# The flipped spectral product in 64 x 64 tiles with two PSUM banks

## The chip, the cores and the metric

The kernel runs on one core of a Trainium2 chip, as one program. The metric is device microseconds of that core from the launch's first to its last work, the median of three runs. TensorE is called PE here, its weight loads PEld, VectorE DVE, ScalarE ACT, GpSimd POOL and SyncE, which issues most DMAs, SP.

## The reference

Two layers on x of shape (4, 128, 64, 64) in float32: four images of 128 channels and 64 x 64 = 4096 tokens. The first layer is attention with four heads of 32 over the 4096 tokens, with projection, residual and a layer norm over the channels. The second takes that result and adds three branches:

```
spatial = conv_general_dilated(x, conv_spatial_w (3x3), padding 1) + bias
ym      = mamba(tokens of x)            # d_inner 256, 16 states, 4 taps
fft     = rfft2(x, axes=(-2, -1))
cat     = concatenate([fft.real, fft.imag], axis=1)
fc      = einsum("bchw,oc->bohw", cat, conv_spectral_w) + conv_spectral_b
fr, fi  = split(fc, 2, axis=1)
spectral = irfft2(complex(fr, fi), s=(h, w), axes=(-2, -1))
return spatial + spectral + ym
```

The spectral branch mixes channels in the frequency domain with a 256 x 256 matrix. Written out in the image domain, it is a channel mix of x, of a Hilbert transform of x along the rows, and of the same two with the image flipped in both directions. The part that goes to flipped positions is the one of this case: for a chunk of tokens, w = g_flip^T x + g_fliphil^T hilbert(x), with two 128 x 128 matrices.

## The kernel before, in words

**Chunks and steps.** The 4 x 4096 tokens are cut into 32 chunks of 512 (8 rows of an image). Attention sets the beat. A loop over t (from L1126 on) walks steps; 2048 of them do attention, 64 per chunk: two pairs of heads, 32 key tiles of 128 each. One step does, for 512 queries and 128 keys of two heads:

- L515 (`scores_for_exp`): the scores into bank pair `s2`, as pairs of matmuls with 64 contraction rows and 128 columns in float32r (one pass of the array), three pairs, the last from `MX`; ACT's exp reads them (L523, `e`).
- L474 (`scores_for_max`): the scores of another step once more into bank pair `s1`, two pairs of the same form; DVE's max reduce reads them (L481, `part`).
- L535 (`times_values`): `po` += V^T e, two matmuls in float32 on 128 rows and 33 columns. A float32 matmul stands in the trace as two MATMUL records (two passes), so this is four.

`s1` and `s2` have one buffer each, so L474 of a step waits for L481 of the step before, and L515 for L523.

**Products.** Everything else that PE does is small float32 products, through the helper `product` (L346): it splits the 128 output rows into two column tiles of 64, so each has 128 contraction rows and 64 columns. All such records carry line L349. PSUM's eight banks are two for `s1`, two for `s2`, one for `po`, one for the scan's `dA`, and two, `m0` and `m1`, which all the small jobs share.

**The planner.** The small jobs are generators. Each `yield` says what the next piece needs: "P" a PE place, "A" an ACT place, "D" a DVE place, "B" one of the two banks, and "" just another step. `Plan.step` (L125) runs in every step of attention; it goes through the jobs in the order of (rank, time, number) and advances each one at most by a piece that takes a bank, then on through pieces that need only "P" if places are left. Odd steps give two places each of P, A and D; even steps give one A place only (L1168, L1170). A bank comes back a step or two after `plan.release`. The engines' queues are in program order, so this order is the order on each engine. In an odd step the plan's products stand between L474 and L535 of that step on PE; on DVE, the jobs' work stands behind the reduce L481. On even steps DVE also does one row of the state scan (L884), POOL two or three multiplies for it.

**The jobs of a chunk.** `output_projection` (rank 0: `pa`, `py`, norm, `xh`), `mamba_input` (rank 1: transposes `pt`, then `xp`), which starts two `scan_input` (rank 1: `pi`, four taps on DVE, a sigmoid), `scan_bc` (rank 1: `pd`), two `scan_dt` (rank -1: `pdt`), `spectral` (rank 2), `gate` and `convolve` (rank 3: `pz`, `pf`), `scan_output` (rank 0: `py`), and the next image's `project_kv` and the next chunk's `project_q` (rank 0: `pk`, `pv`, `pq`). The state scan of a chunk is due 64 steps after its `mamba_input`.

**`spectral` (L925).** It takes a bank and a P place for `p1`, the Hilbert transform of `xh` on PE (tile `p` in the trace); ACT copies it to `hx` (L936). Then it takes a bank and a P place for `pw`: `product` with `g_flip` from the image tile `xp`; a P place, and `product` with `g_fliphil` from `hx` into the same bank. ACT copies the bank to `w` (L947), and SP writes `w` to DRAM (L951), from where `load_flipped` and `add_flipped` (L1010, L1023) take it for other chunks' outputs. `hx` is also read by `convolve`.

**The tail.** Attention ends some 220 us before the end; after it chunks 30 and 31 finish their scans, with more places per step (L1163) and POOL and DVE as the busy engines.

Of the kernel before, what the change touches and what calls it, by code (L numbers as in the profile page):

```python
# [11 lines left out]
AF = mybir.ActivationFunctionType  # L12
ALU = mybir.AluOpType
# [4 lines left out]
P = 128  # L18
W = 64
# [4 lines left out]
L = 512  # L24
RPC = L // W
# [136 lines left out]
def attention_then_conv_mamba(  # L162
# [17 lines left out]
    nc = tc.nc  # L180
    ctx.enter_context(tc.manual_schedule())
    B, C, N = x.shape
# [18 lines left out]
    for h in range(HEADS):  # L201
        k, j = divmod(h, 2)
# [3 lines left out]
    for h in range(HEADS):  # L206
        k, j = divmod(h, 2)
        c = COL["bk"] + k
# [8 lines left out]
    for h in range(HEADS):  # L217
        k, j = divmod(h, 2)
        c = COL["bq"] + h
# [36 lines left out]
    def col(name, k=0):  # L256
        return vec[:, COL[name] + k : COL[name] + k + 1]
# [12 lines left out]
    g_flip, g_hil, g_fliphil = (g[:, k, :] for k in range(3))  # L270
# [70 lines left out]
    rows = [slice(j * HS, (j + 1) * HS) for j in range(2)]  # L341
    used = [slice(j * HS, j * HS + HD + 1) for j in range(2)]

    plan = Plan(2, {"x": 2, "f": 1})

    def product(out, lhsT, rhs, start=True, stop=True):  # L346
        for q in range(2):
            cols = slice(q * HS, (q + 1) * HS)
            nc.tensor.matmul(out[cols], lhsT[:, cols], rhs, start=start, stop=stop)  # L349

    def bank_tile(bank, shape, name):
        return psum.tile(shape, F32, tag=f"m{bank}", name=name)
# [309 lines left out]
    def inner(c):  # L662
        return xps[c][:, 1 : RPC + 1, 1 : W + 1]

    def mamba_input(c):

        i = c % NCH
        while c not in XH:
            yield ""
        yield ""  # L670
        xp = loc.tile([P, RPC + 2, W + 2], F32, tag="xp", name=f"xp_{c}", bufs=2)
        xps[c] = xp
        nc.gpsimd.memset(xp[:, :, 0 : W + 2 : W + 1], 0.0)
        if i == 0:
            nc.gpsimd.memset(xp[:, 0, 1 : W + 1], 0.0)
            nc.gpsimd.memset(carry, 0.0)
        if i == NCH - 1:
            nc.gpsimd.memset(xp[:, RPC + 1, 1 : W + 1], 0.0)
        bank = yield "PB"
        pt = bank_tile(bank, [P, TPC, P], f"pt_{c}")  # L680
        for t in range(TPC):
            nc.tensor.transpose(pt[:, t, :], XH[c][:, t, :], ident)
        yield "A"
        plan.release(bank)
        nc.scalar.activation(
            inner(c),
            pt.rearrange("p t (r w) -> p (t r) w", w=W),
            AF.Identity,
            scale=col("gamma"),
            bias=col("beta"),  # L690
        )
        if i:
            nc.scalar.activation(xp[:, 0, 1 : W + 1], xps[c - 1][:, RPC, 1 : W + 1], AF.Copy)
            nc.scalar.activation(xps[c - 1][:, RPC + 1, 1 : W + 1], xp[:, 1, 1 : W + 1], AF.Copy)
            edges.add(c - 1)
        if i == NCH - 1:
            edges.add(c)

        xss[c], dts[c], us[c] = {}, {}, {}
        for hf in range(NH):  # L700
            plan.now(1, scan_input(c, hf))
        plan.now(2, spectral(c))

    def scan_input(c, hf):

        bank = yield "PB"
        pi = bank_tile(bank, [P, RPC, W], f"pi_{c}_{hf}")
        product(pi, inw[:, hf * P : (hf + 1) * P], inner(c))
        yield "A"
        plan.release(bank)  # L710
        xi = loc.tile([P, L + TAPS - 1], F32, tag=f"sg{hf}", name=f"xi_{c}_{hf}", bufs=1)
        nc.scalar.activation(xi[:, : TAPS - 1], carry[:, hf, :], AF.Copy)
        nc.scalar.activation(xi[:, TAPS - 1 :], pi.rearrange("p r w -> p (r w)"), AF.Identity)
        nc.scalar.activation(carry[:, hf, :], xi[:, L:], AF.Copy)
        s = loc.tile([P, L], F32, tag=f"xs{hf}", name=f"xs_{c}_{hf}", bufs=1)
        bank = yield "DB"
        ps = bank_tile(bank, [P, L], f"conv_{c}_{hf}")
        nc.vector.tensor_scalar(
            ps, xi[:, :L], col("c1_w", hf * TAPS), col("c1_b", hf), ALU.mult, ALU.add
        )  # L720
        for k in range(1, TAPS):
            yield "D"
            nc.vector.scalar_tensor_tensor(
                s if k == TAPS - 1 else ps,
                xi[:, k : k + L],
                col("c1_w", hf * TAPS + k),
                ps,
                ALU.mult,
                ALU.add,
            )  # L730
        plan.release(bank, 2)
        a = yield from sigmoid(s, f"sg{hf}", f"{c}_x{hf}")
        nc.gpsimd.tensor_tensor(s, s, a, ALU.mult)  # L733
        yield ""
        xss[c][hf] = s
        if len(xss[c]) == NH:
            plan.now(1, scan_bc(c))
# [187 lines left out]
    def spectral(c):  # L925

        b, i = divmod(c, NCH)
        bank = yield "PB"
        p1 = bank_tile(bank, [P, TPC, P], f"p1_{c}")
        for t in range(TPC):  # L930
            product(p1[:, t, :], XH[c][:, t, :], hilbert)
        yield "A"
        plan.release(bank)
        hx = loc.tile([P, L], F32, tag="hx", name=f"hx_{c}", bufs=2)
        hxs[c] = hx
        nc.scalar.activation(  # L936
            hx, p1.rearrange("p t c -> p (t c)"), AF.Copy, scale=col("gamma")
        )
        bank = yield "PB"
        pw = bank_tile(bank, [P, RPC, W], f"pw_{c}")  # L940
        product(pw, g_flip, inner(c), True, False)
        yield "P"
        product(pw.rearrange("p r w -> p (r w)"), g_fliphil, hx, False, True)
        yield "A"
        plan.release(bank)
        w = loc.tile([P, L], F32, tag="w", name=f"w_{c}", bufs=1)
        nc.scalar.activation(w, pw.rearrange("p r w -> p (r w)"), AF.Copy)  # L947
        yield ""
        if i == 0:
            wd[b] = dram.tile([P, N], F32, tag="wd", name=f"wd_{b}")  # L950
        nc.sync.dma_start(wd[b][:, i * L : (i + 1) * L], w)  # L951
# [162 lines left out]
    for c in range(CHUNKS):  # L1114
        t0 = (c + 1) * SLOT
        plan.at(t0, 0, load_residual(c))
        plan.at(t0 + 16, 1, mamba_input(c))
        plan.at(t0 + SLOT + 30, 3, convolve(c))
        plan.at(c * SLOT + LAG + 6, 3, gate(c))
        plan.at((c + 1) * SLOT + LAG + (2 if c < CHUNKS - 3 else 6), 0, scan_output(c))  # L1120
# [7 lines left out]
    while t < end or not plan.idle():  # L1128
# [10 lines left out]
        c, s = divmod(t - LAG, SLOT)  # L1139
# [110 lines left out]
```

## Time and profile before

| What | Value |
|---|---|
| Median of 3 runs | 5814.76 us (5813.01 to 5815.22) |
| Profiled execution, its own time | 5816.46 us |
| Span from first to last instruction in it | 5814.7 us |
| Mean granted TensorE clock | 0.986 |
| PE busy / DVE / ACT / POOL | 97% / 75% / 61% / 79% |
| `pw<-xp,g` on PE | 128 records of 632 ns mean |
| `pw<-hx,g` on PE | 128 records of 605 ns mean |
| `w<-pw` on ACT (L947) | 32 of 590 ns |
| `hx<-p` on ACT (L936) | 32 of 684 ns |

The profile is of one execution. A row of groups names line, engine, operation, the tiles out<-in, the tile of the array as contraction rows * columns (64*128), out and in shapes, and the count. PE records overlap, so a group's cost is read from its start to the next group's start.

### The profile page before, as it was taken

To read this page: it belongs to the slowest core of one execution; us is meant where nothing else is said; L and a number is where in the kernel's file an instruction comes from. 1 tells how busy PE (TensorE), PEld (TensorE's weight loads), DVE (VectorE), ACT (ScalarE), POOL (GpSimd) and SP (SyncE) were. 2 spreads that over 40 slices of the span, in tenths; PEclk is the share of its full clock that TensorE was granted. 3 is DMA by queue.
4 is the path that set the end of the run, shared out by engine and by line. 5 is a ranking of instruction groups with operands and counts; after the bars stand their busy time and mean duration, and the time that the engine had idled before them with its cause. 6 is when DMAs were issued, how large, how long until landed. Compare 5 with 4: busy or idle time off the path is not lost. (4 is left out here: it accounts for less than half of the span.)

```text
span 5814.7 us, 89440 instructions
## 1 busy us (share of the span) xinstructions
PE 5614.2 (97%) x33642; PEld 2423.7 (42%) x33642; DVE 4357.9 (75%) x4665; ACT 3518.5 (61%) x4794; POOL 4578.1 (79%) x4659
## 2 busy tenths in 40 slices
PE   5999999999999999999999999999999999999976
PEld 2444444444444444444444444444444444444421
DVE  4557777777777777777777777777777777777768
ACT  1455666666666666666666666666666666666653
POOL 0006888888888888888888888888889888888987
PEclk7999999999999999999999999999999999999988
DMA  4012233333333232333433323332433222232233
GB/s 133 22 32 64 68 76 77 74 73 111 87 94 80 74 73 77 75 71 87 110 89 83 81 69 74 80 76 70 113 78 96 71 69 66 69 73 69 66 98 93
DMA packets 424880, 456.81 MB, mean 79 GB/s; under 512 B 203872, under 2 KB 207488, under 8 KB 424448
## 3 DMA queue, kind: packets, MB, share of 16 engines
q1 hardware_dynamic: 419792, 449.23, 30.9%
q8 instruction: 265, 4.34, 0.3%
q10 hardware_dynamic: 4656, 1.87, 0.1%
q14 instruction: 167, 1.37, 0.1%
HBM read 376.21 MB, written 66.32 MB: 76 GB/s over the span
## 5 line engine op out<-in xcount | busy, mean ns | idle before, releaser
L481 DVE TENSOR_REDUCE part<-s 128x2 f32<-128x1024 f32 x2048 | 2500.7, 1222 | 1300.1 <-PE s L474 1295.7
L523 ACT ACTIVATE e<-s 128x1024 f32<-128x1024 f32 x2048 | 2097.1, 1024 | 1977.9 <-PE s L515 1968.1
L535 PE MATMUL po<-e,V 128*33 128x512 f32 x8192 | 2145.1, 602 | 11.3 <-ACT oz L546 11.3
L515 PE MATMUL s<-Q,K 64*128 64x512 f32 x8192 | 1502.5, 444 | 29.6 <-ACT e L523 26.0
L515 PEld LDWEIGHTS s<-Q,K 64*128 64x128 f32 x8192 | 610.6, 185 | 1754.8 <-ACT e L523 1330.0
L474 PE MATMUL s<-K,Q 64*128 64x512 f32 x8192 | 1309.1, 396 | 30.8 <-DVE part L481 19.3
L894 POOL TENSOR_TENSOR hs<-hs,bc 128x512 f32<-128x512 f32 x948 | 1215.1, 1282 | 138.5 <-DVE hs L884 70.2
L872 POOL TENSOR_TENSOR db<-u,bc 128x512 f32<-128x512 f32 x948 | 1218.1, 1285 | 0.0
L913 POOL TENSOR_TENSOR acc<-acc,hs 128x512 f32<-128x512 f32 x894 | 1146.9, 1283 | 70.1
L884 DVE TENSOR_TENSOR_SCAN hs<-dA,state,db 128x512 f32<-128x512 f32 x826 | 1052.6, 1274 | 51.0 <-ACT dA L867 48.8
L474 PEld LDWEIGHTS s<-K,Q 64*128 64x128 f32 x8192 | 769.1, 185 | 252.2 <-DVE part L481 64.7
L515 PE MATMUL s<-MX,sel 64*128 64x512 f32 x4096 | 814.4, 392 | 0.0
L867 ACT ACTIVATE dA<-dt,negA 128x512 f32<-128x512 f32 x1024 | 702.4, 686 | 91.6 <-DVE V L884 79.2
L535 PEld LDWEIGHTS po<-e,V 128*33 128x33 f32 x8192 | 339.9, 109 | 761.6 <-issue 706.0
L893 POOL COPY state<-hs 128x1 f32<-128x1 f32 x858 | 160.1, 187 | 526.6 <-DVE hs L884 526.1
L515 PEld LDWEIGHTS s<-MX,sel 64*128 64x128 f32 x4096 | 390.5, 184 | 93.6 <-issue 0.4
L349 PE MATMUL pf<-d,cw 128*64 128x256 f32 x1536 | 195.1, 384 | 0.0
L579 POOL TENSOR_TENSOR op<-op,rz 128x512 f32<-128x512 f32 x32 | 41.6, 1299 | 176.6 <-DMA rz<-rd 176.6
L884 DVE TENSOR_TENSOR_SCAN hs<-dA,zero,db 128x512 f32<-128x512 f32 x128 | 163.1, 1274 | 1.2 <-POOL db L872 1.0
L349 PE MATMUL acc<-V,cst 128*64 128x512 f32 x280 | 91.1, 748 | 67.8 <-POOL V L894 67.3
L349 PEld LDWEIGHTS pf<-d,cw 128*64 128x64 f32 x1536 | 102.0, 136 | 100.4 <-issue 59.1
L733 POOL TENSOR_TENSOR xs<-xs,sg_x 128x512 f32<-128x512 f32 x64 | 82.1, 1282 | 74.0 <-ACT sg_x L657 74.0
(158 smaller groups left out, 3455.7 us busy)
## 6 DMA issues: line engine op xcount, KB each, us to landing
bc<-bcd SPq DMA_DIRECT2D x487, 512.0 KB
Q<-qd SPq DMA_DIRECT2D x256, 128.0 KB
K<-kd SPq DMA_DIRECT2D x64, 256.0 KB
MX<-md SPq DMA_DIRECT2D x1024, 0.5 KB
K<-bcd SPq DMA_DIRECT2D x42, 256.0 KB
vd<-vst SPq DMA_DIRECT2D x32, 264.0 KB
V<-vd SPq DMA_DIRECT2D x32, 264.0 KB
xq<-in_x SPq DMA_DIRECT2D x32, 256.0 KB
```

Source lines behind the costliest of these rows:

```text
L349: nc.tensor.matmul(out[cols], lhsT[:, cols], rhs, start=start, stop=stop)
L474: nc.tensor.matmul(sc[:, j, :], QT[H][rows[j], n, t * P : (t + 1) * P], KK[k][m][rows[j], :], start=n == 0, stop=n == 1,)
L481: nc.vector.tensor_reduce(part[H][:, :, t, m], sc, AX.X, ALU.max)
L515: nc.tensor.matmul(s[:, j, :], sel[rows[j], :] if n == 2 else KK[k][i][rows[j], t * P : (t + 1) * P], mov[rows[j], :], start=n == 0, stop= ...
L523: nc.scalar.activation(e, s, AF.Exp)
L535: nc.tensor.matmul(po[H][used[j], :], VA[i][:, t, 2 * k + j, :], e[:, j, :], start=m == 0, stop=m == NT - 1,)
L867: nc.scalar.activation(dA[c, v], dts[c][hf], AF.Exp, scale=negA[:, k : k + 1])
L872: engine.tensor_tensor(db[c, v], us[c][hf], bcs[c, n][0], ALU.mult)
L884: nc.vector.tensor_tensor_scan(hs, dA.pop((c, v)), db.pop((c, v)), state[:, k : k + 1] if c % NCH else zero, ALU.mult, ALU.add,)
L893: nc.gpsimd.tensor_copy(state[:, k : k + 1], hs[:, L - 1 :])
L894: nc.gpsimd.tensor_tensor(hs, hs, bcs[c, n][1], ALU.mult)
L913: nc.gpsimd.tensor_tensor(accs[c, hf], accs[c, hf], hs, ALU.add)
```

## The change

The flipped product no longer goes through `product`. Each of the two factors is cut into two halves of the contraction (rows 0 to 63 and 64 to 127) and two halves of the output columns, so into four tiles of 64 x 64. The two halves of the contraction go into two different banks, `pw[0]` and `pw[1]`; each bank collects both factors. Eight matmuls in all, in the order factor, row half, column half, take the place of four. They are issued together on one P place. ACT copies the first bank to `w` as before, and DVE adds the second bank to `w`, on a D place of its own; `w` goes to DRAM as before. The job asks for its first bank without a place ("B"), keeps it, and asks for the second with the P place ("PB"). Its rank in the planner goes from 2 to 1.

```diff
-        plan.now(2, spectral(c))
+        plan.now(1, spectral(c))
...
-        bank = yield "PB"
-        pw = bank_tile(bank, [P, RPC, W], f"pw_{c}")
-        product(pw, g_flip, inner(c), True, False)
-        yield "P"
-        product(pw.rearrange("p r w -> p (r w)"), g_fliphil, hx, False, True)
-        yield "A"
-        plan.release(bank)
+        banks = [(yield "B"), (yield "PB")]
+        pw = [bank_tile(k, [P, L], f"pw{r}_{c}") for r, k in enumerate(banks)]
+        for first, lhsT, rhs in ((True, g_flip, inner(c)), (False, g_fliphil, hx)):
+            for r in range(2):
+                for q in range(2):
+                    nc.tensor.matmul(
+                        pw[r][rows[q]],
+                        lhsT[rows[r], rows[q]],
+                        rhs[rows[r]],
+                        start=first,
+                        stop=not first,
+                    )
+        yield "A"
+        plan.release(banks[0])
         w = loc.tile([P, L], F32, tag="w", name=f"w_{c}", bufs=1)
-        nc.scalar.activation(w, pw.rearrange("p r w -> p (r w)"), AF.Copy)
+        nc.scalar.activation(w, pw[0], AF.Copy)
+        yield "D"
+        plan.release(banks[1], 2)
+        nc.vector.tensor_tensor(w, pw[1], w, ALU.add)
```

## The prediction

> **What bounds the kernel now.** I read the page's busy shares and its 40 slices first:
>
> ```profile
> PE 5614.2 (97%) x33642; PEld 2423.7 (42%) x33642; DVE 4357.9 (75%) x4665; ACT 3518.5 (61%) x4794; POOL 4578.1 (79%) x4659
> PE   5999999999999999999999999999999999999976
> DVE  4557777777777777777777777777777777777768
> PEclk7999999999999999999999999999999999999988
> ```
>
> PE is at 90% or more in every slice but the first and the last two; DVE has about a quarter free in between. A busy PE may still be waiting behind itself, so I went to PE's timeline around one product that the change touches:
>
> ```profile
> 1084.37 0.63 PE L474 MATMUL s<-K,Q 64*128 64x512 f32 x4
> 1084.92 1.05 PE L535 MATMUL po<-e,V 128*33 128x512 f32 x4
> 1085.91 0.73 PE L515 MATMUL s<-Q,K 64*128 64x512 f32 x4
> 1086.48 0.39 PE L515 MATMUL s<-MX,sel 64*128 64x512 f32 x2
> 1086.71 0.63 PE L474 MATMUL s<-K,Q 64*128 64x512 f32 x4
> 1087.27 1.08 PE L349 MATMUL pw<-xp,g 128*64 128x512 f32 x4
> 1088.18 1.03 PE L349 MATMUL pw<-hx,g 128*64 128x512 f32 x4
> 1089.04 1.03 PE L535 MATMUL po<-e,V 128*33 128x512 f32 x4
> 1089.99 0.73 PE L515 MATMUL s<-Q,K 64*128 64x512 f32 x4
> 1090.57 0.40 PE L515 MATMUL s<-MX,sel 64*128 64x512 f32 x2
> 1090.80 0.63 PE L474 MATMUL s<-K,Q 64*128 64x512 f32 x4
> ```
>
> The first number is the start. Read start to start, because the ends overlap the next group. One attention step, from an L474 group to the next, is 1086.71 - 1084.37 = 2.34 us; the step with the two `pw` products is 1090.80 - 1086.71 = 4.09 us. So the flipped product costs 4.09 - 2.34 = 1.75 us of PE, with no gap in it. Of 32 chunks, 31 run it in such a step (the last one, at 5670 us, is in the tail): 31 x 1.75 = 54 us, 0.9% of the time, is all that the PE side can give. Last, PE's own waits on other engines inside these steps:
>
> ```profile
> PE s L515 <- ACT e L523: 26.0, 49, 0.8
> PE s L474 <- DVE part L481: 19.3, 29, 1.3
> PE po L535 <- ACT oz L546: 11.3, 35, 0.3
> ```
>
> That is 57 us in all, 1.8 us per chunk: attention steps are bound by PE's own throughput, not by waits.
>
> **Part 1, the rate inside the product.** `pw<-hx` takes 0.86 us to the next group (1089.04 - 1088.18) with four records of about 0.59 us each: two column tiles, each f32 matmul in two passes. Two tiles run side by side: the records start in pairs (1087.268 and 1087.275, then 1087.749 and 1087.756), so one pass of 512 columns is 0.86 / 2 = 0.43 us, whatever the number of tiles beside it. After the change, each of the two factors is four tiles of 64 x 64, eight records. Row halves side by side are shown by L515 and L474 (two 64-row tiles per pair), column halves by L349; both at once by no row. If all four run together, a factor is again 2 x 0.43 = 0.86 us: the same arithmetic on the same array. If only two at a time, it is 1.72 us, +1.72 us for both factors. If a 64-row tile streamed a pass in half the time, it would be 0.43 us, -0.86 us for both. I take four together: both halvings are seen separately, and the array is fully covered before and after, so no cells lie idle that the new tiles could use. A small loss: the L515 `MX` pair, row tiles with 512 columns in one pass, takes 1086.71 - 1086.48 = 0.23 us, against 0.215 per half-length of a column pass (0.86 / 4). If row tiles lose this 0.015 us in each of the four passes, that is 0.06 us per chunk.
>
> [...]
>
> **Part 2, the change of tile shape.** The timeline has a price for it. Two pairs of L474 alone are 2 x 0.23 = 0.46 us, but from L474 to `pw` it is 1087.27 - 1086.71 = 0.56: 0.10 us for the change. The first `pw` group then takes 0.91 instead of 0.86: 0.05 us of weight load with nothing to hide it. From `pw` to `po`, both 128-row column tiles, nothing is paid (0.86); into `po` from `s` it costs 0.99 - 0.86 - 0.10 (the exit) = 0.03 of weight load and 0.10 of change. So now there are two changes a step, s to pw and po to s. With 64 x 64 tiles there are three: s to pw, pw to po, po to s. The added one is 0.10 + 0.03 = 0.13 us per chunk. Bounds: if `s` to 64 x 64 is no change, because both have 64 rows, 0.15 us goes and this term is -0.02; if another product comes ahead of `pw` in its step (the P place that the change frees allows it), one more change of 0.15 is added: +0.28. I take 0.13: every pair of unlike shapes that stand next to each other in this trace pays.
>
> [...]
>
> **Part 3, the eviction.** Removed: nothing on ACT (one copy of 128x512 before, L947, 590 ns, and one after, from bank 0). Added on DVE: a 128x512 add of PSUM and SBUF. The same form is in the trace:
>
> ```profile
> L1061 DVE TENSOR_TENSOR ob<-ym,py 128x512 f32<-128x512 f32 x32 | 21.7, 678 | 2.8 <-PE py L349 2.8
> ```
>
> So 0.68 us x 32 = 22 us on DVE, which goes from 75% to 75.3%. What hides it is DVE's idle time ahead of the reduce that frees the max scores' bank:
>
> ```profile
> 1093.82 1.23 DVE L481 TENSOR_REDUCE part<-s 128x2 f32<-128x1024 f32 x1
> 1094.96 0.68 DVE L655 SCALAR_TENSOR_TENSOR sg_z<-zg,ln_z 128x512 f32<-128x512 f32 x1
> 1097.05 1.23 DVE L481 TENSOR_REDUCE part<-s 128x2 f32<-128x1024 f32 x1 [1.42 <-PE s L474]
> ```
>
> In the very step after the `pw` eviction DVE does one 0.68 us job and then idles 1.42 us; a second one fits. Behind the add, if its wait for PE or ACT ran late, stand that reduce and, behind the reduce, PE's next L474. Where the add meets a full DVE (the plan lets two D jobs into one odd step), all 0.68 us reach PE: 31 x 0.68 = 21 us. From below: 0. I take 0, with 0.7 us for the one chunk in the tail, where DVE is busy 93.9 of the last 114 us. The write of `w` to DRAM now waits on DVE instead of ACT; behind it on SP's queue are Q and bc loads issued steps ahead of use, so I cost this at nothing; a late one would show as a PE wait, of which L474 on Q has 0.7 us now.
>
> **Part 4, banks and order.** The plan has two banks for all small jobs. The spectral job now takes one, keeps it while it waits for the other, and then holds both until ACT and DVE have read them: for two to four steps no other bank job starts. Its rank goes from 2 to 1, so it passes `scan_bc`, and it needs one P place fewer. This moves jobs by steps, but the state scan of a chunk is due 64 steps after its `pt` (L1117 and LAG), and in the trace `pd` and the last `pdt` come 65 and 83 us after `pt` (1093.7 and 1111.4 against 1028.4), some 24 and 31 steps at the 172.6 us from one `pt` to the next; so none should come late. What a move can do is put an ACT or DVE job beside or away from a full step. Now that costs PE, per chunk, 26.0 / 32 = 0.8 us at L515 and 19.3 / 32 = 0.6 at L474. One wait of about 0.7 us more or less per chunk is 31 x 0.7 = 22 us up or down. I take 0: no row says which.
>
> **The sum.** Per chunk 0.06 + 0.13 = 0.19 us; 31 x 0.19 = 5.9, with 0.7 in the tail 6.6 us. The profiled execution took 5816.5 us (span 5814.7): 5823.1. The median of the runs is 1.7 lower, 5814.76, so the forecast is 5821 us, +0.1%.
>
> **Rivals.**
> - *Slower, two tiles at a time* (the change doesn't do what it says): +1.72 x 31 + 6.6 = +60 us, 5875. For it: no row has four tiles at once. Against: paired starts for both halvings. It decides as soon as the four first-pass records of a factor don't start within a few tens of ns. Chance 0.12.
> - *Slower, DVE or the banks become a wait of PE* in about every chunk: 0.4 to 1 us x 31 on top of the sum, +19 to +38, about 5843. For it: L474 waits for DVE already 29 times, once per chunk. Chance 0.17.
> - *Faster, the moved jobs take away one of PE's waits*: -22 + 6.6 = -15, 5800. Chance 0.08.
> - *Faster, a 64-row pass is half as long*: -0.86 x 31 + 6.6 = -20, 5795. Chance 0.03; nothing speaks for it but that L474's 64-row passes take 0.23, and those also make one pass where these f32 products make two.
> - *The forecast*, +0 to +11 us: chance 0.60.
>
> A difference under 0.2% (11.6 us) is about what a measurement of this kernel can't tell from none. Faster 0.11, within 0.60, slower 0.29. The forecast's own range is 5810 to 5826. From 5794 to 5852 the range takes in both faster cases and nearly all of the DVE one; left out are the two-at-a-time case and little else.
>
> **What the profile after would show.** Part 1: sixteen `pw` records per chunk, form 64*64, each group of eight 0.85 to 0.95 us to the next; 1.7 means two at a time. Part 2: `po` after `pw` starting 0.1 late and its first pass 0.03 longer; the step with `pw` at about 4.28 instead of 4.09. Part 3: a new DVE group of 32 at 0.68 us, and PE's wait for L481 still near 19 us. Part 4: PE's wait for L523 still near 26 us. The prediction is wrong if one of the last two moves by more than 10 us, or if the `pw` groups aren't 0.9 us.

## The result, and the profile after

The changed kernel takes 5869.64 us (5867.65 to 5872.63), against 5814.69 before (four runs): ratio 1.0095, 95% interval 1.008 to 1.011. The forecast was 5821, its range ended at 5852. The profiled execution took 5871.4 us, 55.0 more than that of before. The page after, the same lines as before:

```profile
PE 5643.0 (96%) x33898; PEld 2422.4 (41%) x33898; DVE 4374.3 (75%) x4697; ACT 3516.2 (60%) x4794; POOL 4572.5 (78%) x4659
PE   6999999999999999999999999999999999999976
PEclk7999999999999999999999999999999999999988
```

PE has 256 records more (8 per chunk) and only 29 us more of busy time; its share even fell. So the page says little; the timeline says more. First PE around one changed product (the x4 line is the same place in a window cut 0.4 us behind its start):

```profile
1100.40 0.63 PE L474 MATMUL s<-K,Q 64*128 64x512 f32 x4
1100.96 1.09 PE L944 MATMUL pw<-xp,g 64*64 64x512 f32 x8
1101.87 1.03 PE L944 MATMUL pw<-hx,g 64*64 64x512 f32 x8
1102.84 1.05 PE L535 MATMUL po<-e,V 128*33 128x512 f32 x4
```

```profile
1100.96 0.66 PE L944 MATMUL pw<-xp,g 64*64 64x512 f32 x4
```

Four records start at once (1100.959 to 1100.979 singly), and each factor of eight records takes 0.91 and 0.97 us to the next group, where before had 0.91 and 0.86. So all four tiles run together, and nothing is seen of a cost of row tiles. The exit into `po` shows the added change of shape: 0.97 - 0.86 = 0.11. The add on DVE, by group, and where it falls in time:

```profile
L957 DVE TENSOR_TENSOR w<-pw,w 128x512 f32<-128x512 f32 x32 | 21.9, 683 | 3.6 <-ACT w L954 2.3 <-PE pw L944 1.3
```

```profile
1109.47 0.68 DVE L957 TENSOR_TENSOR w<-pw,w 128x512 f32<-128x512 f32 x1
1110.88 1.23 DVE L481 TENSOR_REDUCE part<-s 128x2 f32<-128x1024 f32 x1 [0.73 <-PE s L474]
```

Behind this add DVE still idles 0.73 us. So neither the tiles nor, in this step, the add is where 55 us went. PE's waits on others point elsewhere (us in total, times, longest):

```profile
PE s L515 <- ACT e L523: 42.4, 105, 0.7
PE po L535 <- ACT oz L546: 20.3, 63, 0.3
PE s L474 <- DVE part L481: 18.6, 28, 1.3
```

Against 26.0, 49 times, and 11.3, 35 times, before: about twice as many waits for the exp and for `oz`. `oz` is the copy of a finished `po`, which happens at each change of head pair, every 32 steps. By the steps in which they fall, before has 29 of the waits for the exp and 30 of those for `oz` behind the second change of a chunk (steps 33 and 34), and 0 and 3 behind the first. After has the same behind the second and adds 56 and 27 behind the first (steps 1 to 3). Here is the first step behind such a change at the start of a chunk (step 1 of its 64): PE before, ACT before, then PE, ACT and DVE after:

```profile
1994.99 0.74 PE L515 MATMUL s<-Q,K 64*128 64x512 f32 x4
1995.56 0.40 PE L515 MATMUL s<-MX,sel 64*128 64x512 f32 x2
1995.79 0.63 PE L474 MATMUL s<-K,Q 64*128 64x512 f32 x4
1996.35 1.08 PE L349 MATMUL pf<-hx,g 128*64 128x512 f32 x4
1997.26 1.03 PE L349 MATMUL pf<-d,cw 128*64 128x256 f32 x8
1998.12 1.03 PE L535 MATMUL po<-e,V 128*33 128x512 f32 x4
1999.08 0.73 PE L515 MATMUL s<-Q,K 64*128 64x512 f32 x4
```

```profile
1996.10 0.59 ACT L546 ACTIVATE oz<-po 33x512 f32<-33x512 f32 x1 [1.27 <-DVE oz L545]
1997.11 1.01 ACT L523 ACTIVATE e<-s 128x1024 f32<-128x1024 f32 x1
```

```profile
2011.71 0.73 PE L515 MATMUL s<-Q,K 64*128 64x512 f32 x4
2012.27 0.40 PE L515 MATMUL s<-MX,sel 64*128 64x512 f32 x2
2012.51 0.62 PE L474 MATMUL s<-K,Q 64*128 64x512 f32 x4
2013.47 1.05 PE L535 MATMUL po<-e,V 128*33 128x512 f32 x4 [0.33 <-ACT oz L546]
2014.89 0.73 PE L515 MATMUL s<-Q,K 64*128 64x512 f32 x4 [0.37 <-ACT e L523]
```

```profile
2012.82 0.59 ACT L546 ACTIVATE oz<-po 33x512 f32<-33x512 f32 x1 [1.40 <-DVE oz L545]
2013.32 0.58 ACT L802 ACTIVATE lnw<-u 128x512 f32<-128x512 f32 x1
2013.84 1.00 ACT L523 ACTIVATE e<-s 128x1024 f32<-128x1024 f32 x1
```

```profile
2010.84 1.23 DVE L481 TENSOR_REDUCE part<-s 128x2 f32<-128x1024 f32 x1 [2.01 <-PE s L474]
2012.09 0.70 DVE L545 COPY oz<-po 33x512 f32<-33x512 f32 x1
```

Read it from the bottom. DVE copies its half of `po` only behind a reduce (2012.09), ACT's half waits for that (2012.82), PE's next `po` waits for ACT (2013.47, 0.40 later than the usual 0.56 behind L474), and the exp, third in ACT's queue, holds the next L515 by 0.43. Before, two products of the convolution (`pf`, 1.75 us of PE) stood in just this step: the copy ended at 1996.69, well ahead of PE's `po` (1998.12), and the exp at 1998.12, ahead of the next L515 (1999.08), so nothing waited. After, the products aren't there.

**Where the 55 us are.** For every attention step I took the time from its first L515 record to the next step's, and took off the price of what stands in it: 2.348 us for the step and 0.87 to 0.885 per product, the medians of steps without waits. The sum of what is left over (the excess, us, from chunk 1 on; "K" are other steps with over 0.8 us each):

| Steps of the 64 in a chunk | before | after |
|---|---|---|
| 0 to 2, first change of head pair | 5.3 | 36.0 |
| 32 to 34, second change of head pair | 33.6 | 33.6 |
| K, mostly the load of a new image's keys, three times | 10.1 | 19.4 |
| the `pw` step itself | -0.5 | 3.7 |
| all others | 12.9 | 21.2 |
| sum | 61.4 | 113.9 |

Of the 52.5 us between the sums, 30.7 are the first line. (PE's two wait lines above grew by 25 only: they count from the modelled end of the record before, start to start counts all.) Another 2.7 us come in the tail; no cause is known for them. The order of the products tells the reason of the first line. Steps in which they stand in PE's queue, from 49 on into the next chunk (so in 21 of the 31 chunks; before, step 1 holds two products in 28 of the 31, after in none):

```
before  49 pw  51 pd  53 pf+pf  55 pdt+pf  57 pdt  61 pz           1 pf+pf  3 pq+pf   5 pf
after   53 pw  55 pd  57 pz     59 pdt+pdt         61 pf+pf 63 pf  7 pq    11 pf+pf  13 pa+pf  15 pf
```

In the plan of after, which the planner's code gives without a run, the spectral job takes its first bank in step 49, where before it issued `pw`; the second is held by the gate's logarithm until 52, so `pw` comes in 53. `pd` goes from 51 to 55, `pz` passes the convolution, the convolution starts eight steps late, and step 1 stays empty. The rank alone does nothing of this: in the plan with only the rank changed, PE's instructions stand in the same order as before (no run was made of it).

### The profile page after: what moved, and what is told of

Read it like the earlier page. It is cut to its first block, busy times and chain, and to the rows that moved or that the text cites. A ratio compares the mean times of both kernels' runs of the same rounds, so it can differ in the third digit from the quotient of the medians.

```text
span 5869.6 us, 89999 instructions
## 1 busy us (share of the span) xinstructions
PE 5643.0 (96%) x33898; PEld 2422.4 (41%) x33898; DVE 4374.3 (75%) x4697; ACT 3516.2 (60%) x4794; POOL 4572.5 (78%) x4659
## 5 line engine op out<-in xcount | busy, mean ns | idle before, releaser
L481 DVE TENSOR_REDUCE part<-s 128x2 f32<-128x1024 f32 x2048 | 2499.4, 1221 | 1273.2 <-PE s L474 1269.4
L523 ACT ACTIVATE e<-s 128x1024 f32<-128x1024 f32 x2048 | 2093.4, 1022 | 1983.9 <-PE s L515 1980.1
L535 PE MATMUL po<-e,V 128*33 128x512 f32 x8192 | 2147.8, 603 | 20.5 <-ACT oz L546 20.3
L515 PE MATMUL s<-Q,K 64*128 64x512 f32 x8192 | 1503.6, 445 | 47.5 <-ACT e L523 42.4
L474 PE MATMUL s<-K,Q 64*128 64x512 f32 x8192 | 1313.2, 398 | 34.6 <-DVE part L481 18.6
L515 PEld LDWEIGHTS s<-Q,K 64*128 64x128 f32 x8192 | 611.1, 185 | 1779.4 <-ACT e L523 1327.7
L872 POOL TENSOR_TENSOR db<-u,bc 128x512 f32<-128x512 f32 x948 | 1215.3, 1282 | 0.0
L884 DVE TENSOR_TENSOR_SCAN hs<-dA,state,db 128x512 f32<-128x512 f32 x826 | 1053.1, 1275 | 106.2 <-POOL db L872 59.9
L474 PEld LDWEIGHTS s<-K,Q 64*128 64x128 f32 x8192 | 767.8, 186 | 267.4 <-DVE part L481 74.5
L515 PE MATMUL s<-MX,sel 64*128 64x512 f32 x4096 | 813.6, 393 | 0.0
L515 PEld LDWEIGHTS s<-MX,sel 64*128 64x128 f32 x4096 | 388.0, 184 | 93.0 <-issue 0.6
L884 DVE TENSOR_TENSOR_SCAN hs<-dA,zero,db 128x512 f32<-128x512 f32 x128 | 163.2, 1275 | 7.9 <-POOL db L872 7.7
```

The source lines that it names most:

```text
L474: nc.tensor.matmul(sc[:, j, :], QT[H][rows[j], n, t * P : (t + 1) * P], KK[k][m][rows[j], :], start=n == 0, stop=n == 1,)
L481: nc.vector.tensor_reduce(part[H][:, :, t, m], sc, AX.X, ALU.max)
L515: nc.tensor.matmul(s[:, j, :], sel[rows[j], :] if n == 2 else KK[k][i][rows[j], t * P : (t + 1) * P], mov[rows[j], :], start=n == 0, stop= ...
L523: nc.scalar.activation(e, s, AF.Exp)
L535: nc.tensor.matmul(po[H][used[j], :], VA[i][:, t, 2 * k + j, :], e[:, j, :], start=m == 0, stop=m == NT - 1,)
L872: engine.tensor_tensor(db[c, v], us[c][hf], bcs[c, n][0], ALU.mult)
```

## The experiments

Theory A: the moved order leaves attention's own waits at a change of head pair without work to cover them; the tiles cost 4 us. Rivals: B, the 64 x 64 shape is the cost; C, the DVE add is; D, the bank kept idle is, wherever the products stand. The kernel before was run again beside each set of experiments (medians 5815.12 us for 1 to 4, 5815.9 for 5 to 8, 5816.55 for 9 and 10); the ratios are to these.

**1. Old tile shape in the new order.**

```diff
+        product(pw[0].rearrange("p (r w) -> p r w", w=W), g_flip, inner(c))
+        product(pw[1], g_fliphil, hx)
```

in place of the loop of eight matmuls.

> The kernel after, with its two banks, its places, its rank and its DVE add, but with the old tile shape: the factor g_flip goes into the first bank and g_fliphil into the second, each through the helper in tiles of 128 rows by 64 columns. Theory A (lost cover: the moved order of the small products leaves attention's own waits open, and the tile shape itself costs 0.13 us per chunk): 5870 less 31 x 0.13 = 4, about 5866. Theory B (the 64 x 64 shape is what costs): back near 5815 to 5820. Theory C (the DVE add or the reads of two banks cost): 5866 as in A, so this run doesn't part A from C.

Measured 5861.61 us, ratio to before 1.0078 (1.0063 to 1.0093). B falls: with the old tiles 47 of the 55 us stay. The first line of the table is 35.7, the `pw` step -0.5 again. From the first to the last attention step it is 4.8 us less than after, 4.2 of them in the `pw` step, which is the tiles; the other 3 us of the difference of medians lie in the tail and ahead of the first step, and I have no cause for them.

**2. The cover taken away from before.**

```diff
-            plan.step(t, {"D": 2, "P": 2, "A": 2})
+            plan.step(t, {"D": 2, "P": 0 if t % SLOT == 1 else 2, "A": 2})
```

> The kernel before, with nothing changed but that the plan gives no PE place in step 1 of every chunk's 64 (t % 64 == 1), the odd step behind the change of head pair; the convolution's product that stood there moves to step 3. No work is added. Theory A: the wait at that step opens, about the 31 us by which the excess over the sum of the products grew at that step from before to after: 5840 to 5848. Theory B and C: 5815 within 5.

Measured 5845.77 us, ratio 1.0052 (1.0037 to 1.0067). Before, with its one bank, its tiles and no added work, is 31 us slower when step 1 has no product. The excess at steps 0 to 2 goes from 5.3 to 36.7, that at all others stays. This is A's mechanism by itself.

**3. Products moved into the two steps, in after.** The same line of the plan, with `0 if t % NT == NT - 1 else 2`.

> The kernel after, with 64 x 64 tiles and two banks, but the plan gives no PE place in the last odd step ahead of each change of head pair (t % 32 == 31). That moves one convolution product from step 63 to step 1 and one input product from step 31 to step 33. No work is removed. Theory A: each stands in a wait of about 1.1 us with 0.88 us of PE work, so 0.7 to 0.9 us comes back at each of the two steps: 31 x 2 x 0.8 = 50, about 5820. Theory B and C: 5870 within 5, since tiles, eviction and amount of work are the same.

Measured 5826.01 us, ratio to before 1.0018 (1.0009 to 1.0028): 44 us back, with tiles, banks and add as in after. A expected 50. PE at step 1 and the step behind it now:

```profile
1994.93 0.62 PE L474 MATMUL s<-K,Q 64*128 64x512 f32 x4
1995.49 1.08 PE L349 MATMUL pf<-d,cw 128*64 128x256 f32 x8
1996.40 1.03 PE L535 MATMUL po<-e,V 128*33 128x512 f32 x4
1997.36 0.74 PE L515 MATMUL s<-Q,K 64*128 64x512 f32 x4
1998.72 1.05 PE L535 MATMUL po<-e,V 128*33 128x512 f32 x4
1999.97 0.50 PE L515 MATMUL s<-Q,K 64*128 64x512 f32 x2 [0.19 <-ACT e L523]
```

One product of 0.88 us covers the first wait, and a second, 0.19 us, stays a step later. Excess 36.0 to 21.0 at steps 0 to 2, 33.6 to 4.5 at 32 to 34. The miss against A's 50 is mostly in steps 0 to 2: in ten of the 31 chunks (the first three and the last seven) no product came into step 1, which leaves 7.9 us, and step 2 keeps 8.3.

**4. The same rule in before.**

> The kernel before with the same rule (no PE place where t % 32 == 31). Only the input product moves, from step 31 to step 33, where before has an open wait of about 1.1 us in each chunk (33.6 us in all). Theory A: 31 x 0.8 = 25 us faster, about 5790. Theory B and C say nothing of it: 5815.

Measured 5787.63 us, ratio 0.9952 (0.9938 to 0.9967): 27 us faster than before. The second change of head pair had been open in both kernels; 33.6 goes to 4.6.

**5. Both banks in one piece**, up to chunk 22. The planner learns a need with two B's and serves it when two banks are free (its own lines are left out here):

```diff
-        banks = [(yield "B"), (yield "PB")]
+        if c < CHUNKS - NCH - 1:
+            banks = yield "PBB"
+        else:
+            banks = [(yield "B"), (yield "PB")]
```

> The kernel after, but up to chunk 22 the flipped product takes its two banks in one piece, when both are free, instead of keeping the first for four steps while it waits for the second. By the plan it then runs in step 49, as before, and the input of the scan follows in step 51; but the convolution still comes late, and step 1 of a chunk still holds no product. Theory A (what counts is which steps hold a product): the wait behind step 1 stays, about 31 us, and only the smaller waits go, of which the load of K (9 us) is the largest: 5850 to 5862. Theory D (the bank kept idle is the cost, wherever the products come to stand): about three quarters of the 50 us go, 5830 or less.

Measured 5845.05 us, ratio 1.0049 (1.0034 to 1.0064), 5 us under A's range and 15 above D's. Steps 0 to 2 keep 34.8 us, as A said, since `pz` and not the convolution comes last and step 1 is empty still. The K line went from 19.4 to 8.9 and the others fell by 10, more than I had counted. So taking the first bank early costs about 24 us, through these and 4 us of the tail, and is not the cause of the largest part.

**6. Both copies of `po` on ACT**, in after.

```diff
-            nc.vector.tensor_copy(oz[H][used[1], :], p[used[1], :])
+            nc.scalar.activation(oz[H][used[1], :], p[used[1], :], AF.Identity)
```

> The kernel after, with both halves of po copied to oz by ACT (L545 moves from DVE to ACT). The order of the products is untouched. If the open wait behind a change of head pair is the chain reduce on DVE, copy on DVE, copy on ACT, PE's next po and ACT's next exp, then ACT's two copies of 0.59 us start as soon as po ends, po is free about 0.3 us sooner, and the exp about as much: 31 x 2 x 0.3 to 0.5 = 19 to 31 us faster than after, 5839 to 5851. If the wait has another source (the load of Q, the P places), 5870 within 5.

Measured 5838.37 us, ratio 1.0037 (1.0024 to 1.005), 31 us faster than after. Both changes of head pair lose about 12 us (36.0 to 23.6, 33.6 to 21.9), and the wait of `po` for `oz` is all but gone from PE's lines (20.3 to 0.3). So DVE's late copy is about a third of the excess. What is left is PE's wait for the exp, which didn't fall (42.4 to 42.6): in the step that I read, at 1828 us, the exp stands behind both copies and L802 on ACT, and PE's next L515 waits 0.38 us for it. The other 7 us came in smaller waits, 5 of them in step 12.

**7. The add left out.** The line of the DVE add is taken away, its place in the plan stays.

> The kernel after with the DVE add left out, so that w holds only one half of the contraction; the place for it in the plan and both banks' times are kept. Theory A: the add lies in DVE's idle time, 5870 within 4. Theory C: the add is the cost, about 5820 to 5830.

Measured 5869.24 us, ratio 1.0089 (1.0074 to 1.0104): as after. C falls, and the 22 us of DVE work cost nothing.

**8. Experiment 4 with both copies on ACT.**

> The kernel before with no PE place where t % 32 == 31, as in the run that was 27 us faster than before, and both copies of po on ACT. Each change of head pair has a product in its wait now, so little is left for the second edit: 5780 to 5788.

Measured 5784.16 us, ratio 0.9944 (0.9927 to 0.996). That is 3 us under experiment 4, which was run in another set; the two intervals overlap, so nothing is shown of a second gain. As expected, what is covered has little left to give.

**9 and 10. The whole cover given back to after.** The plan's line once more, with no P place in steps 61 and 63, and in the second kernel none in 31 either.

> The kernel after, with no PE place in steps 61 and 63 of a chunk's 64, so that the two first convolution pieces (1.75 us of PE work) move together into step 1, the one behind the change of head pair where before had 1.74 us of products. No work is removed; nothing of the tiles, banks or the add is touched. Theory A: the wait of step 1 is covered wholly, as before: 30 of the 36 us there come back, 5836 to 5842. Theory B, C: 5870 within 5.

> As the run before it, and with no PE place in step 31 either, which moves one input product into step 33. Theory A: 30 us at step 1 and 29 us at step 33 come back: 5807 to 5813, at or under the kernel before, with the change still in.

Measured 5832.3 us (ratio 1.0026, 1.0016 to 1.0035) and 5810.46 us (0.9987, 0.9978 to 0.9997). In the first, PE at step 1:

```profile
1997.97 0.62 PE L474 MATMUL s<-K,Q 64*128 64x512 f32 x4
1998.53 1.95 PE L349 MATMUL pf<-d,cw 128*64 128x256 f32 x16
2000.30 1.03 PE L535 MATMUL po<-e,V 128*33 128x512 f32 x4
2001.26 0.73 PE L515 MATMUL s<-Q,K 64*128 64x512 f32 x4
```

No wait is left there: 36.0 goes to 6.2, nearly the 5.3 of before, and the total by 37 us, some 7 of it in smaller waits (step 12 above all), more than expected. With the second step covered too, the kernel with the change in it is a little faster than before, though not than experiment 4, which is before with that step covered: it is 23 us slower than that. Part of the 23 is that in the last seven chunks step 1 is empty in this kernel (excess at steps 0 to 2 14.8, against 6.2 in experiment 9). With experiment 2, this settles the cause of the largest part.

## Why the prediction was wrong, point by point

- **The step that failed is Part 4**, "Banks and order": "One wait of about 0.7 us more or less per chunk is 31 x 0.7 = 22 us up or down. I take 0: no row says which." A row did say. I asked of each moved product only whether its reader would get it in time; I didn't ask what it had covered where it stood. The trace of before shows the same change of head pair twice per chunk, with 1.1 us of waits at step 33, where no product stands, and in 28 of the 31 chunks none at step 1, where two do: 33.6 against 5.3 us. Step 33, before:

```profile
1045.21 0.62 PE L474 MATMUL s<-K,Q 64*128 64x512 f32 x4
1046.15 1.05 PE L535 MATMUL po<-e,V 128*33 128x512 f32 x4 [0.32 <-ACT oz L546]
1047.88 0.73 PE L515 MATMUL s<-Q,K 64*128 64x512 f32 x4 [0.67 <-ACT e L523]
```

  That is the price of an empty step, and the order after says that step 1 is empty. It was 30.7 us, some 40% more than the 22 that I had as the far end of one wait.
- **Averages per chunk hid it.** Part 4 spread the totals evenly: 0.8 us at L515 and 0.6 at L474. The waits for the exp do come once per chunk, but in one place, at the end of step 33 (29 of the 49, 19.5 of the 26.0 us; the others lie in the last chunk). Those for L481 don't, though I wrote so among the rivals: of the 29 (19.3 us), 27 lie in the first 300 us, in chunk 0:

```profile
PE s L474 <- DVE part L481: 18.1, 27, 1.3
```

- **The same step of the prediction, second size:** the load of a new image's keys, in steps 51 and 52, three times: 8.6 us before, 18.0 after. The 1.75 us of `pw` had stood two steps ahead of it, so before, PE came to the load later; in experiment 5, with `pw` in step 49 again, the K line is back at 8.9. PE's waits for K themselves grew from 6.1 to 10.8; the rest, 4.7 us, is near the estimate of some 5 us for the time at a granted clock of 0.50 (last section).
- **Not all readers were in time.** After, DVE's state scan (L884) waits for POOL's products (L872) 67.6 us in 44 places, before 1.5 in 2. In step 12 this reaches PE, through the reduce behind the scan: an excess of 7.6 us there, 0.1 before. The longest, DVE then PE:

```profile
3092.51 1.28 DVE L884 TENSOR_TENSOR_SCAN hs<-dA,state,db 128x512 f32<-128x512 f32 x1 [3.61 <-POOL db L872]
3094.97 0.73 PE L474 MATMUL s<-K,Q 64*128 64x512 f32 x4 [1.23 <-DVE part L481]
```

  Why POOL comes late there is open, and a few us in other steps (6, 50) weren't traced singly.
- **The forecast's sign** rested on Parts 1 and 2, and these held: but they make 4 of the 55 us, so that the sign came out right is mostly luck. Four tiles at once: right. +0.19 us per chunk expected; the `pw` step took 4.222 us against 4.086, so 0.136 us. The 0.06 for row tiles was too much, the change of shape at 0.13 about right (0.11 in the timeline).
- **Part 3** was right: the add costs nothing (experiment 7). That L481's wait stayed (19.3 to 18.6) says less than I thought, since most of it lies ahead of the steps in question.
- **The rivals.** "DVE or the banks become a wait of PE" came nearest, at 0.4 to 1 us per chunk on top of the sum; it was about 1.6. The banks did it, through the order; the wait that it named as a sign, L474's for DVE, wasn't the one. It was closed off at 38 us because I priced it by what PE waits for now per line, not by the waits that are covered now. The time fell near "two tiles at a time" (5875), whose mechanism is shown wrong by the four starts within 20 ns: the time alone would have pointed to the wrong cause.
- The test that I had named, L523's wait moving by more than 10 us, is the one that failed: 26.0 to 42.4.

## What to carry to other kernels

On a saturated engine a filler job has a second use: the stall that it stands in. When a change moves such a job, look at each place that it leaves, find the same place elsewhere in the trace without a filler, and price the hole by that. A resource taken early and kept while waiting for a second one shifts everything behind it, and the order of the queue, not the amount of work, is then the thing to predict.

## What the runs showed of the hardware

Four float32 matmuls in tiles of 64 x 64 ran together in the changed product: at 1100.96 us their first passes start 7 ns apart, and the second passes follow 0.48 us later in the first factor and 0.43 in the second, the same as with two tiles of 128 x 64 before.

One wait was followed by more loss than its own length. After, PE stands still for 3.08 us at the first new image's keys, and the granted clock falls to 0.50:

```profile
1447.20 1.22 PE L474 MATMUL s<-K,Q 64*128 64x512 f32 x4 [3.08 <-DMA K<-kd]
1448.35 1.92 PE L535 MATMUL po<-e,V 128*33 128x512 f32 x4
```

The next view gives four stretches from there: length, PE busy (records), granted clock, DMA share, GB/s:

```profile
1443.70:1447.20 3.50, 0.42 (x5) 0.86 0.75 232
1447.20:1450.20 3.00, 3.00 (x8) 0.50 0.49 188
1450.20:1453.80 3.60, 3.60 (x18) 0.61 0.16 61
1454.00:1460.00 6.00, 6.00 (x44) 1.00 0.19 49
```

`po` takes 1.85 us to the next group instead of 0.99; the clock stands at 0.50 for 6.8 us in all (1446.2 to 1453.0). From chunk 1 to the end of attention it dropped once before (3.4 us) and three times after (6.8, 6.8 and 3.4 us, 17 together). Half of the added 13.7 us, less the 3.1 us of it in which PE stood anyway, is some 5 us of the loss, an estimate, inside the K line and its neighbours.

The length of the wait alone doesn't decide it. After, waits of 3.08, 3.96 and 3.80 us for a new image's keys (to 1447.20, 2847.78 and 4247.79) came with the three drops, which began 2.1 and 1.8 us into the first two and 0.7 us behind the third. Before, 2.87 us (to 2823.79) were followed by the one drop, and 1.15 us (to 1439.53) and 2.12 us (to 4208.59) by none. But 1.55 us in experiment 4 (to 1432.69) were followed by 3.4 us at half clock, and 2.82 us in experiment 3 (to 1438.26) by none. What sets the drop isn't shown by these runs.
